# Third graph layer: other PSUM banks for the sums, another place for the keys, weights made in two parts, one more step in a tile's end

## The chip, the cores and the metric

The kernel runs on one core of a Trainium2 chip. The metric is the device time of one execution in microseconds; the kernel before has 2208.41 us, the median of three runs (2205.49 to 2208.99). The profile was taken in an execution of 2205.02 us whose span, from the first to the last instruction, is 2203.2 us. Times of day below, such as "1681.4", are microseconds from the start of that span.

## The reference

Four layers run one after the other over 4096 nodes with 128 features and one adjacency matrix of 4096 x 4096; each adds its result to x and normalises. The third and fourth (L2 and L3 of the reference) are the ones around the change:

```python
# layer 1: attention with 4 heads over adj, its output goes into x
x = _layernorm(x + _L1_gnn_ref(x, adj, Wq, bq, Wk, bk, Wv, bv, Ws, bs, Wb), axis=-1)

# layer 2: graph convolution
adj_hat = adj + eye(n)
d = (adj_hat.sum(1) + 1e-08) ** -0.5
x = _layernorm(x + relu(((d[:, None] * adj_hat * d[None, :]) @ x) @ weight))

# layer 3: graph attention with one head
H = x @ W.T + b
s, r = H @ a_s, H @ a_r
e = leaky_relu(A * s + A * r.T, 0.2)
att = softmax(where(A > 0, e, NEG), axis=1)
x = _layernorm(x + att @ H)
```

## The kernel before, in words

`layer1` is the attention. It keeps, in a pool `keep1` of SBUF, the values `VA` (17,024 bytes in a partition), the keys `KS` (64 KB), two buffers of queries `QS` and one of adjacency, `at0`, in this order. Its work is in one of two branches of a run-time If: `attention_unshifted`, which runs with these inputs, or `attention_shifted`. In the first, a step is one block of 128 keys against 512 queries: PE makes scores (L900), ACT the exponentials (L907), DVE masks them (L909), PE sums with the values (L926), the sums two steps behind the scores. When the 32 blocks of a tile of 512 queries are done, `ending` finishes the tile in pieces: ACT copies the two sums from PSUM (L939), PE transposes (L949), DVE and ACT do the rest and write `Y`, the scaled x of the tile (L1009). The last tile's `ending` has no scores beside it.

`layers23` follows at once. It opens a pool `ring` of 64 KB with eight slots of 1 MB of adjacency each, at the same SBUF address at which `keep1` began, then `keep3` and others behind it. Its PSUM pools `ps_a`, `ps_b`, `ps_t`, `ps_s` have two banks each, in this order from bank 0. In layer 1's branch that ran, `ps_s` (scores and the transposes `pto`) has banks 0 to 5 and `ps_v` (the sums) banks 6 and 7. In the other branch they belong to `ps_big` (0 to 3), `ps_t` (4 to 6) and `ps_o` (7), the last one for the sum `po`.

The loop over `groups` is written out by hand (`manual_schedule`), so the order in the code is the order on each engine. A block g is one slot of the ring; I = g // 8 is the tile of 512 output columns, J = g % 8 the block in it. For I < 8, `convolve` puts Y through the identity into the sum `pa` at J = 0 (L1254) and then adds four products with the block (L1260, two PE passes each, 8 matmuls in the trace). For J < 4, DVE also counts entries that are neither 0 nor 1 (`odd`, L1268). For the ninth tile, `attend_first` begins layer 3: DVE makes four weights `w` a block (L1280, four buffers) and PE sums them with `F` (L1283) into `pa3`.

Two pieces of work lie between the blocks. `weights`, after block 2, prepares layer 3's matrices: PE makes `pu` (L1224, L1225) and turns the weights into `pw` (L1234), DVE copies them out (L1228 to L1236), PE multiplies the copy by `last` into the same bank (L1237), DVE writes `wx`, `tot`, `eps` (L1238 to L1241). `finish(I)` ends tile I while tile I + 1 runs. It is a generator: its first piece, the copy of `pa` (L1297), goes out at J = 7, the others at J = 0, 1, 3, 5 and 6 of the next tile, after that block's own work:

- J = 0: product with the layer's weights (L1301), Relu on ACT (L1304), x + o on DVE (L1305), statistics, Ln and Exp of the variance (L1309, L1310)
- J = 1: normalisation of the four row groups (L1314)
- J = 3: transposes on PE (L1320), copy on ACT (L1321), `XB` on DVE (L1322)
- J = 5: products `pr` and `psr` (L1326, L1330), DVE and ACT make `rho` and `col`
- J = 6: `F` on ACT and DVE (L1344, L1345)

At the end of the loop `close_first` tests the ranges, PE adds the constant to `pa3` (L1386), ACT copies it to `a0` (L1387), the PSUM pools are closed, and a second If takes `attend_factored`. It opens `ps_a3` (two banks from 0) and `ps_b3` and runs layer 3 for the other seven tiles: PE L1425 opens a sum, DVE L1434 makes the `w`, PE L1437 adds.

A framework places tiles and pools and writes every semaphore wait itself: a new tile in reused memory waits for what used the memory before.

Of the kernel before, what the change touches and what calls it, by code (L numbers as in the profile page):

```python
# [10 lines left out]
F32R = mybir.dt.float32r  # L11
# [3 lines left out]
PSUM = bass.MemoryType.PSUM  # L15

P = 128
# [25 lines left out]
class Net:  # L43
# [701 lines left out]
    def layer1(self, Wq, bq, Wk, bk, Wv, bv, Ws, bs, Wb, R):  # L745
# [4 lines left out]
        nc, tc, N, NT, D, X = self.nc, self.tc, self.N, self.NT, self.D, self.X  # L750
        NH, C = 4, D // 4
        with ExitStack() as ctx:
            self.on_scalar = 4
            keep = ctx.enter_context(tc.tile_pool(name="keep1", bufs=1))

            VA = keep.tile([P, NT * NH * (C + 1) + 32], F32, tag="VA", name="VA")
            V = VA[:, 0 : NT * NH * (C + 1)].rearrange("p (t h c) -> p t h c", t=NT, h=NH)
            KS = keep.tile([P, NH, N], F32R, tag="KS", name="KS")
            QS = [keep.tile([P, NH, S], F32R, tag=f"QS{k}", name=f"QS{k}") for k in range(2)]
            at0 = keep.tile([P, 4, S], F32, tag="at0", name="at0")  # L760
            nc.scalar.dma_start(out=at0, in_=self.adjT[0, 0])
# [20 lines left out]
            with ExitStack() as pctx:  # L782
# [10 lines left out]
                for c in range(NC):  # L793
                    s = slice(c * S, (c + 1) * S)
                    for a, w, bias in ((1, wk, bkc), (0, wq, bqc)):
                        p = self.ps_t.tile([P, S], F32, tag="pt", name="pqk")
# [12 lines left out]
                for g in self.groups():  # L809
                    p = self.ps_t.tile([P, 4, P], F32, tag="pt", name="pt")  # L810
# [8 lines left out]
                for g in self.groups():  # L819
                    p = self.ps_t.tile([P, 4, P], F32, tag="pt", name="pt")  # L820
# [13 lines left out]
                p = self.ps_t.tile([P, S], F32, tag="pt", name="pb")  # L834
# [341 lines left out]
    def layers23(self, w2, weight, bias, a_s, a_r, out, Y):  # L1176
# [6 lines left out]
        with ExitStack() as ctx:  # L1183
# [3 lines left out]
            pctx = ctx.enter_context(ExitStack())  # L1187
# [9 lines left out]
            pre = pctx.enter_context(tc.tile_pool(name="pre3", bufs=1))  # L1197
            rot = pctx.enter_context(tc.tile_pool(name="rot2", bufs=2))
            wp = pctx.enter_context(tc.tile_pool(name="w2", bufs=4))
            ps_a = pctx.enter_context(tc.tile_pool(name="ps_a", bufs=2, space=PSUM))  # L1200
            ps_b = pctx.enter_context(tc.tile_pool(name="ps_b", bufs=2, space=PSUM))
            ps_t = pctx.enter_context(tc.tile_pool(name="ps_t", bufs=2, space=PSUM))
            ps_s = pctx.enter_context(tc.tile_pool(name="ps_s", bufs=2, space=PSUM))
            w = self.load_mat(w2, "w2")
            br = self.load_row(bias, "br3", keep)
            wn = self.load_mat(weight, "wn3", pre)
# [14 lines left out]
            def weights():  # L1221

                p = ps_t.tile([P, 4, P], F32, tag="pt", name="pu")
                nc.tensor.matmul(p[:, 0, 0:2], lhsT=wn, rhs=ac[:, 0:2], start=True, stop=True)  # L1224
                nc.tensor.matmul(  # L1225
                    p[:, 1, 0:2], lhsT=ac[:, 2:3].to_broadcast([P, P]), rhs=ac[:, 0:2], start=True, stop=True
                )
                nc.vector.tensor_copy(us, p[:, 0, 0:1].to_broadcast([P, P]))  # L1228
                nc.vector.tensor_copy(ur, p[:, 0, 1:2])
                nc.vector.tensor_copy(cb, p[:, 1, 0:2])  # L1230


                p = ps_t.tile([P, 4, P], F32, tag="pt", name="pw")
                nc.tensor.transpose(p[:, 0, :], wn, self.ident)  # L1234
                nc.vector.tensor_copy(wt, p[:, 0, :])
                nc.vector.tensor_copy(last, self.ident[:, D - 1 : D].to_broadcast([P, P]))  # L1236
                nc.tensor.matmul(p[:, 1, :], lhsT=last, rhs=wt, start=True, stop=True)  # L1237
                nc.vector.tensor_tensor(wx[:, 0:D], wt, p[:, 1, :], ALU.subtract)  # L1238
                nc.vector.tensor_copy(wx[:, D : D + 1], self.ident[:, D - 1 : D])
                nc.vector.memset(tot[:, D - 1 : D], float(N))  # L1240
                nc.vector.memset(eps, TINY)  # L1241
# [45 lines left out]
            def finish(I):  # L1287


                s, tl = slice(I * S, (I + 1) * S), slice(4 * I, 4 * I + 4)  # L1290
                x = X[:, tl, :]
                a = rot.tile([P, S], F32, tag="a", name="a")
                o = rot.tile([P, 4, D], F32, tag="o", name="o")
                rs = rot.tile([P, 4], F32, tag="rs", name="rs")
                XT = rot.tile([P, S], F32, tag="XT", name="XT")
                r = rot.tile([P, 4], F32, tag="r", name="r")
                nc.scalar.copy(a, st["pa"])  # L1297
                yield
                pb = ps_b.tile([P, 4, D], F32, tag="pb", name="pb")
                for b in range(4):  # L1300
                    nc.tensor.matmul(pb[:, b, :], lhsT=a[:, b * P : (b + 1) * P], rhs=w, start=True, stop=True)  # L1301
                for b in range(4):
                    t = 4 * I + b
                    nc.scalar.activation(o[:, b, :], pb[:, b, :], AF.Relu, scale=d[:, t : t + 1])  # L1304
                nc.vector.tensor_tensor(x, x, o, ALU.add)  # L1305
                for b in range(4):
                    self.row_stats(4 * I + b)
                nc.vector.tensor_scalar(rs, self.mv[:, tl, 1], EPS_LN, None, op0=ALU.add)
                nc.scalar.activation(rs, rs, AF.Ln)  # L1309
                nc.scalar.activation(rs, rs, AF.Exp, scale=-0.5)  # L1310
                yield
                for b in range(4):
                    t = 4 * I + b
                    nc.vector.tensor_scalar(  # L1314
                        X[:, t, :], X[:, t, :], self.mv[:, t, 0:1], rs[:, b : b + 1], op0=ALU.subtract, op1=ALU.mult
                    )
                yield
                p = ps_t.tile([P, 4, P], F32, tag="pt", name="pt")
                for b in range(4):
                    nc.tensor.transpose(p[:, b, :], X[:, 4 * I + b, :], self.ident)  # L1320
                nc.scalar.activation(XT, p.rearrange("p a b -> p (a b)"), AF.Identity, accum_out=part[:, I : I + 1])  # L1321
                nc.vector.tensor_tensor(XB[:, tl, :], x, br.unsqueeze(1).to_broadcast([P, 4, D]), ALU.add)  # L1322
                yield
                pr = ps_s.tile([P, S], F32, tag="ps", name="pr")
                for b in range(4):
                    nc.tensor.matmul(  # L1326
                        pr[:, b : b + 1], lhsT=XT[:, b * P : (b + 1) * P], rhs=ur, start=True, stop=True
                    )
                ps = ps_s.tile([P, S], F32, tag="ps", name="psr")
                nc.tensor.matmul(ps, lhsT=us, rhs=XT, start=True, stop=True)  # L1330

                nc.vector.tensor_scalar(r, pr[:, 0:4], cb[:, 1:2], 2.0 * LIMIT, op0=ALU.add, op1=ALU.min)
                nc.vector.tensor_scalar(r, r, -2.0 * LIMIT, None, op0=ALU.max)
                nc.vector.tensor_reduce(mx[:, I : I + 1], r, AX.X, ALU.max, apply_absolute_value=True)
                nc.vector.tensor_scalar(rho[:, s], ps, cb[:, 0:1], 2.0 * LIMIT, op0=ALU.add, op1=ALU.min)
                nc.vector.tensor_reduce(
                    mx[:, NS + I : NS + I + 1], rho[:, s], AX.X, ALU.max, apply_absolute_value=True
                )
                nc.scalar.activation(col[:, 0, tl], r, AF.Exp, scale=-0.8)
                nc.scalar.activation(col[:, 1, tl], r, AF.Exp)  # L1340
                nc.scalar.activation(rho[:, s], rho[:, s], AF.Exp, scale=0.8)
                yield
                for t in range(4 * I, 4 * I + 4):
                    nc.scalar.activation(F[:, t, 0 : D - 1], X[:, t, 0 : D - 1], AF.Copy, scale=col[:, 1, t : t + 1])  # L1344
                nc.vector.tensor_copy(F[:, tl, D - 1], col[:, 1, tl])  # L1345
# [19 lines left out]
            with tc.manual_schedule():  # L1365
                nc.scalar.preload_act_table_set("natural_log_exp_and_others")
                for g in range(RING - 1):
                    load(g)
                for g in range(groups):
                    I, J = g // NS, g % NS  # L1370
                    if I < NS:
                        convolve(I, J)
                    else:
                        attend_first(J)
                    load(g + RING - 1)
                    if g == 2:
                        weights()

                    if J in (0, 1, 3, 5, 6):
                        next(rest, None)  # L1380
                    if J == NS - 1 and I < NS:
                        rest = finish(I)
                        next(rest)
                    if g == groups - 2:
                        close_first()
                nc.tensor.matmul(st["pa3"], lhsT=tot, rhs=eps, start=False, stop=True, skip_group_check=True)  # L1386
                nc.scalar.copy(a0, st["pa3"])  # L1387
# [166 lines left out]
```

## Time and profile before

The stretches of the span around the change, from the profile's windows:

| stretch, us | what runs | PE busy, us | DVE busy, us | ACT busy, us | granted clock |
|---|---|---|---|---|---|
| 1660 to 1680 | last blocks of layer 1 | 15.93 | 17.01 | 10.83 | 1.00 |
| 1680 to 1700 | `ending` of the last tile, blocks 0 to 2 of layer 2 | 14.77 | 13.83 | 0.92 | 0.83 |
| 1700 to 1720 | `weights`, blocks 3 to 7 | 17.79 | 7.45 | 0.00 | 0.91 |
| 1745 to 1936 | tiles 1 to 7 of layer 2 | 191.00 | 91.87 | 45.22 | 1.00 |
| 1936 to 1985 | `attend_first` with `finish(7)` | 40.93 | 31.79 | 9.54 | 0.93 |
| 1985 to 2203.2 | `attend_factored` | 209.12 | 185.91 | 7.61 | 0.99 |

A row is read like this: in the 191 us from 1745 on, PE had a matmul in flight all the time, DVE was busy for less than half of it. The granted clock is the share of TensorE's full speed that the chip gave; at 0.5 every matmul takes twice as long. Over the whole span PE is busy 88%, DVE 85%, ACT 67%.

### The profile page before, as it was taken

To read this page: it belongs to the slowest core of one execution; us is meant where nothing else is said; L and a number is where in the kernel's file an instruction comes from. 1 tells how busy PE (TensorE), PEld (TensorE's weight loads), DVE (VectorE), ACT (ScalarE), POOL (GpSimd) and SP (SyncE) were. 2 spreads that over 40 slices of the span, in tenths; PEclk is the share of its full clock that TensorE was granted. 3 is DMA by queue.
4 is the path that set the end of the run, shared out by engine and by line. 5 is a ranking of instruction groups with operands and counts; after the bars stand their busy time and mean duration, and the time that the engine had idled before them with its cause. 6 is when DMAs were issued, how large, how long until landed. Compare 5 with 4: busy or idle time off the path is not lost.

```text
span 2203.2 us, 24053 instructions
## 1 busy us (share of the span) xinstructions
PE 1944.5 (88%) x8720; PEld 1051.3 (48%) x8720; DVE 1881.1 (85%) x2732; ACT 1474.4 (67%) x1858; POOL 97.8 (4%) x146
## 2 busy tenths in 40 slices
PE   4588888888888708999999999999997999989998
PEld 4376666666666505333333333333333444434443
DVE  6799999999999887789999999999897344558887
ACT  5799999999999774787777787877883222210000
POOL 2000000000000322210000000000000000000000
PEclk7799999999999857999999999999999999999999
DMA  3466665667566307885646565565455777667883
GB/s 93 139 225 224 207 225 202 232 211 247 207 210 215 116 1 248 215 227 174 203 158 187 174 201 178 173 191 176 169 195 222 293 269 272 254 235 275 290 297 112
DMA packets 112868, 448.44 MB, mean 204 GB/s; under 512 B 9760, under 2 KB 20064, under 8 KB 71776
## 3 DMA queue, kind: packets, MB, share of 16 engines
q1 hardware_dynamic: 94160, 361.82, 46.4%
q10 hardware_dynamic: 9360, 68.16, 9.1%
q0 software_dynamic: 9216, 16.78, 4.2%
q8 instruction: 73, 1.20, 0.2%
q14 instruction: 59, 0.48, 0.1%
HBM read 369.10 MB, written 77.63 MB: 203 GB/s over the span
## 4 chain that ended last, share of the span: by engine, by line
PE 40%; DVE 33%; ACT 20%; issue 5%; DMA 2%; ACTq 0%; POOL 0%; SPq 0%; DVEq 0%; POOLq 0%
PE pv L926 10%; PE pa L1260 10%; PE pa L1437 9%; DVE e L909 8%; PE ps L900 6%; ACT e L907 3%; ACT w L612 3%; DVE w L620 3%; DVE t L603 2%; DVE nat L890 2%; DVE w L652 2%; DVE t L648 2%; ACT at L584 2%; ACT y L630 2%; DVE w L663 2%
## 5 line engine op out<-in xcount | busy, mean ns | idle before, releaser
L909 DVE SCALAR_TENSOR_TENSOR e<-at,e 128x2048 f32<-128x2048 f32 x256 | 583.0, 2287 | 69.3 <-ACT e L907 68.6
L907 ACT ACTIVATE e<-ps 128x1024 f32<-128x1024 f32 x512 | 493.1, 1024 | 145.8 <-PE ps L900 126.0
L926 PE MATMUL pv<-e,VA 128*64 128x512 f32 x2048 | 495.8, 605 | 6.7 <-DVE e L909 6.3
L900 PE MATMUL ps<-QS,KS 128*128 128x512 f32 x1024 | 312.9, 424 | 5.1 <-ACT e L907 2.9
L900 PEld LDWEIGHTS ps<-QS,KS 128*128 128x128 f32 x1024 | 171.0, 189 | 230.7 <-ACT e L907 175.1
L926 PEld LDWEIGHTS pv<-e,VA 128*64 128x64 f32 x2048 | 124.7, 136 | 248.7 <-issue 214.3
L1260 PE MATMUL pa<-ring,Y 128*128 128x512 f32 x512 | 228.0, 599 | 1.4 <-DMA wn<-in_L_gnn_W_dram 1.4
L580 PE MATMUL ptA<-ident,ad 128*128 128x128 f32 x1024 | 158.8, 284 | 51.4 <-ACT at L584 48.2
L1437 PE MATMUL pa<-w,F 128*128 128x512 f32 x448 | 195.3, 594 | 0.0
L1434 DVE SCALAR_TENSOR_TENSOR w<-rho,col,ring 128x512 f32<-128x512 f32 x224 | 162.8, 748 | 24.0 <-PE pa L1437 11.3
L580 PEld LDWEIGHTS ptA<-ident,ad 128*128 128x128 f32 x1024 | 120.6, 144 | 130.0 <-ACT at L584 95.8
L596 PE MATMUL pz<-HT 128*128 128x512 f32 x288 | 152.2, 631 | 24.3 <-DVE w L663 15.8
L675 PE MATMUL pi<-HA,w 128*128 128x129 f32 x1152 | 158.6, 284 | 0.0
L1260 PEld LDWEIGHTS pa<-ring,Y 128*128 128x128 f32 x512 | 96.9, 193 | 115.1 <-issue 114.8
L675 PEld LDWEIGHTS pi<-HA,w 128*128 128x128 f32 x1152 | 146.5, 200 | 2.7 <-issue 2.3
L620 DVE TENSOR_TENSOR w<-w,at 128x2048 f32<-128x2048 f32 x64 | 146.4, 2287 | 0.5 <-ACT at L584 0.5
L1437 PEld LDWEIGHTS pa<-w,F 128*128 128x128 f32 x448 | 83.7, 190 | 106.1 <-issue 79.2
L881 ACT ACTIVATE nat<-nat 128x2048 f32<-128x2048 f32 x64 | 122.6, 1915 | 3.8 <-DMA nat<-in_adj_dram 3.7
L690 PE MATMUL pj<-HA,w 128*128 128x129 f32 x896 | 109.5, 274 | 2.4 <-DVE w L663 2.4
L603 DVE SCALAR_TENSOR_TENSOR t<-ei,de,pz 128x512 f32<-128x512 f32 x144 | 104.1, 745 | 6.8 <-DMA ei<-rows 6.7
L690 PEld LDWEIGHTS pj<-HA,w 128*128 128x128 f32 x896 | 104.6, 191 | 2.6 <-DVE w L663 2.6
L658 PE MATMUL ptz<-ident,t 128*128 128x128 f32 x448 | 69.8, 283 | 31.9 <-DVE w L663 22.9
(359 smaller groups left out, 2456.6 us busy)
## 6 DMA issues: line engine op xcount, KB each, us to landing
ring<-adjT SPq DMA_DIRECT2D x128, 1024.0 KB, 5.1
ad<-in_adj_dram SPq DMA_DIRECT2D x64, 1024.0 KB, 5.3
adjT<-at SPq DMA_DIRECT2D x64, 1024.0 KB, 5.0
nat<-in_adj_dram ACTq DMA_DIRECT2D x64, 1024.0 KB, 4.9
at<-adjT SPq DMA_DIRECT2D x63, 1024.0 KB, 4.8
qk<-cut SPq DMA_DIRECT2D x16, 512.0 KB, 11.7
KS<-qk POOLq DMA_DIRECT2D x32, 256.0 KB, 7.1
QS<-qk POOLq DMA_DIRECT2D x32, 256.0 KB, 5.3
```

The source lines that it names most:

```text
L580: nc.tensor.transpose(pt[:, ib, :], ad[:, ib, jb * P : (jb + 1) * P], self.ident)
L596: nc.tensor.matmul(pz, lhsT=HT[:, j * P : (j + 1) * P], rhs=HT[:, I * S : (I + 1) * S], start=True, stop=True)
L620: nc.vector.tensor_tensor(w, w, st[p][f"at{k}"], ALU.mult)
L675: nc.tensor.matmul(row[I, "po"][ib // 2][:, ib % 2, :], lhsT=st[p]["w0"][:, jb, ib * P : (ib + 1) * P], rhs=HA[:, 4 * J + jb, :], start=False,
L690: nc.tensor.matmul(pj[:, a, :], lhsT=st[p]["w1"][:, ib, jb * P : (jb + 1) * P], rhs=HA[:, 4 * I + ib, :], start=(ib == 0), stop=(ib == 3),)
L900: nc.tensor.matmul(p[:, h, :], lhsT=KS[:, h2 + h, jb * P : (jb + 1) * P], rhs=QS[I % 2][:, h2 + h, :], start=True, stop=True,)
L907: nc.scalar.activation(e[:, h2 : h2 + 2, :], p, AF.Exp)
L909: nc.vector.scalar_tensor_tensor(e, at[:, jb % 4, :].unsqueeze(1).to_broadcast([P, NH, S]), 0.0, e, op0=ALU.not_equal, op1=ALU.mult,)
L926: nc.tensor.matmul(st["po"][h // 2][g : g + 64, :], lhsT=VA[:, o : o + 64], rhs=e[:, h, :], start=(jb == 0), stop=(jb == NT - 1), skip_gro ...
L1260: nc.tensor.matmul(st["pa"], lhsT=Y[:, 4 * J + jb, :], rhs=at[:, jb, :], start=False, stop=(J == NS - 1 and jb == 3), skip_group_check=True,)
L1434: nc.vector.scalar_tensor_tensor(w, rho[:, I * S : (I + 1) * S], col[:, 0, j : j + 1], at[:, jb, :], op0=ALU.max, op1=ALU.mult)
L1437: nc.tensor.matmul(pa, lhsT=F[:, j, :], rhs=w, start=False, stop=(j == NT - 1), skip_group_check=True)
```

## The change

There are four edits. In layer 1, `KS` is allocated ahead of `VA`, so that the ring of adjacency afterwards lies over the keys, whose last use is before that of the values. In `layers23` the pool of the sums, `ps_a`, comes last of the four PSUM pools, so it has banks 6 and 7, and layer 3's `ps_a3`, again from bank 0, no longer lies over it. `weights` is cut in two: what needs PE's second product goes into `weights_last`, after block 4, with other blocks between the copies and the product. `finish` gets one more `yield`, after the Relu, so that DVE's part of the first piece comes one block later; the pieces now go out at J = 0, 1, 2, 3, 5 and 6.

```diff
@@ layer1
             keep = ctx.enter_context(tc.tile_pool(name="keep1", bufs=1))
+            KS = keep.tile([P, NH, N], F32R, tag="KS", name="KS")
             VA = keep.tile([P, NT * NH * (C + 1) + 32], F32, tag="VA", name="VA")
...
-            KS = keep.tile([P, NH, N], F32R, tag="KS", name="KS")
@@ layers23
-            ps_a = pctx.enter_context(tc.tile_pool(name="ps_a", bufs=2, space=PSUM))
             ps_b = pctx.enter_context(tc.tile_pool(name="ps_b", bufs=2, space=PSUM))
             ps_t = pctx.enter_context(tc.tile_pool(name="ps_t", bufs=2, space=PSUM))
             ps_s = pctx.enter_context(tc.tile_pool(name="ps_s", bufs=2, space=PSUM))
+            ps_a = pctx.enter_context(tc.tile_pool(name="ps_a", bufs=2, space=PSUM))
@@ weights
                 nc.vector.tensor_copy(last, self.ident[:, D - 1 : D].to_broadcast([P, P]))
+                st["pw"] = p
+
+            def weights_last():
+                p = st["pw"]
                 nc.tensor.matmul(p[:, 1, :], lhsT=last, rhs=wt, start=True, stop=True)
                 nc.vector.tensor_tensor(wx[:, 0:D], wt, p[:, 1, :], ALU.subtract)
@@ finish
                     nc.scalar.activation(o[:, b, :], pb[:, b, :], AF.Relu, scale=d[:, t : t + 1])
+                yield
                 nc.vector.tensor_tensor(x, x, o, ALU.add)
@@ the loop over groups
                     if g == 2:
                         weights()
-
-                    if J in (0, 1, 3, 5, 6):
+                    if g == 4:
+                        weights_last()
+
+                    if J in (0, 1, 2, 3, 5, 6):
                         next(rest, None)
```

## The prediction

> **What bounds the kernel now.** I read the page first: PE is busy 88% and leads the chain of waits with 40% of the span, DVE follows with 33%. Such shares mix stages, so I then asked for stretches of the part that the diff touches, from the end of layer 1 (about 1676 us) to the end.
>
> ```profile
> 1697.60:1702.20 4.60, 0.01 (x1) 0.00 (x0) 4.52 (x9) 0.00 (x0) 0.00 (x0) 0.99 1.01 422
> 1702.20:1705.60 3.40, 3.39 (x6) 1.84 (x7) 2.51 (x5) 0.00 (x0) 0.00 (x0) 0.51 1.01 424
> 1745.00:1936.00 191.00, 191.00 (x571) 94.81 (x572) 91.87 (x179) 45.22 (x110) 0.00 (x0) 1.00 0.72 267
> 1936.00:1950.50 14.50, 9.95 (x31) 4.74 (x29) 6.12 (x18) 5.48 (x13) 0.00 (x0) 1.00 0.65 250
> 1950.50:1962.60 12.10, 12.10 (x25) 5.20 (x26) 11.27 (x19) 1.01 (x2) 0.00 (x0) 0.86 0.60 204
> ```
>
> After the length come PE, PEld, DVE, ACT and POOL busy, then the granted clock. Most of layer 2 (1745 to 1936) has no PE gap: no edit can win there unless it shortens PE's own work, and none does. What can be won lies in the seams: 4.6 us without PE at 1697.6, the hole before 1950.5, and the stretches right behind both, where the clock is 0.51 and 0.86. The timeline names the waits at the first seam:
>
> ```profile
> 1677.41 0.32 SPq L1244 DMA_DIRECT2D ring<-adjT  x1
> ...
> 1681.41 1.83 PE L1254 MATMUL pa<-ident,Y 128*128 128x128 f32 x8 [3.97 <-DVE junk L967]
> ...
> 1684.67 12.43 PE L1260 MATMUL pa<-ring,Y 128*128 128x512 f32 x24 [1.42 <-DMA wn<-in_L_gnn_W_dram]
> ...
> 1687.49 0.21 ACT L994 ACTIVATE rs<-rs 128x4 f32<-128x4 f32 x1
> ...
> 1702.21 0.80 PE L1237 MATMUL pw<-wtr,last 128*128 128x128 f32 x2 [4.60 <-DVE last L1236]
> ...
> 1702.80 18.70 PE L1260 MATMUL pa<-ring,Y 128*128 128x512 f32 x40
> ```
>
> and at the seam between layers 2 and 3:
>
> ```profile
> 1947.14 0.69 DVE L1305 TENSOR_TENSOR X<-X,o 128x512 f32<-128x512 f32 x1 [8.17 <-ACT o L1304]
> ...
> 1949.68 2.74 DVE L1280 SCALAR_TENSOR_TENSOR w<-rho,col,ring 128x512 f32<-128x512 f32 x4
> ...
> 1950.48 12.26 PE L1283 MATMUL pa<-w,F 128*128 128x512 f32 x24 [4.55 <-DVE w L1280]
> ...
> 1962.59 0.60 PE L1320 MATMUL pt<-ident,X 128*128 128x128 f32 x4
> ...
> 1985.70 0.58 ACT L1387 COPY a<-pa 128x512 f32<-128x512 f32 x1 [5.45 <-PE pa L1386]
> ...
> 1986.38 1.09 PE L1425 MATMUL pa<-eps,tot 1*128 1x512 f32 x2 [0.72 <-ACT a L1387]
> ```
>
> The brackets hold the idle time before a piece and what ended it. Strange is the first one: L1254 reads Y and the identity, yet waits for `junk`, which it never touches. I come back to that.
>
> **What the Trainium skill says.** "TensorE: Matmul & The Clock Gate", Part 1: the clock drops to half after an idle window of about 3.4 us and comes back after a busy one, and the windows run freely. The trace agrees: 0.51 for the 3.4 us after the 4.6 us gap, and the weight loads of L1260 there stand 0.85 us apart instead of 0.43. So a gap of PE costs itself plus about 1.7 us. "PSUM: Partial Sum Buffer", section "Engine vs sequencer instructions": the queues of ScalarE and VectorE are strict FIFO. Agreed: the `w` of L1280 stand behind L1305 for 8.17 us with nothing to wait for themselves. "Runtime: NRT & Kernel Launch", section "Instruction fetch mechanics": a taken branch to a far target stalls for the fetch. The trace has PE's branch at the end of layer 1's If with 3.47 us from 1676.8, so PE is free at 1680.3; what it then waits for is a semaphore.
>
> **The change part by part.**
>
> *Keys ahead of values in `keep1`.* `ring` then covers exactly KS, whose last reader is the last L900 (ends 1669.5), and no more VA, read by L926 until 1676.1. If the first ring load waited for just what lies below it, it could go some 7.8 us earlier than 1677.41. But the wait list of that load, in the instructions that the framework emitted for the kernel before, also holds the last read of `at0` and the loads of QS0 and QS1. Those lie beyond 140352 bytes, the ring between 57792 and 123328. So the wait is for the whole pool `keep1`, VA with it, in whatever order the tiles lie. Also, PE needs ring[0] only at 1683.24 (1681.41 + 1.83); earlier landing could win 1.42 at most. I take 0; both ends: 0 and -1.4.
>
> *PSUM order.* `ps_a` moves from banks 0 and 1 to 6 and 7; `ps_b`, `ps_t`, `ps_s` move down by two. At layer 3's entry `ps_a3` lies in banks 0 and 1, until now those of `pa3`, which a0's copy (L1387) still reads. In the new order they are `ps_b`'s, idle since 1946. PE's wait of 0.72 before L1425 goes: -0.7, on PE's path, since layer 3 has PE busy 209 of 218 us.
>
> At layer 2's entry it is the other way round. The waits after the If are the larger of what its two branches ask: L1254 waits for DVE ticks that in the other branch, `attention_shifted`, are the last writes of Y, and in the branch that ran happen to be `junk` (L967). That explains the odd bracket, and the first ring load waiting for `pto` (L949), which in the other branch is VA's last reader. Bank 7 is, in that branch, `po`, last read by a ScalarE copy with tick 1473. In the branch that ran, tick 1473 is L994, which ends at 1687.70. Banks 0 and 1 have no such reader. So L1254 must wait until about 1687.8 instead of 1681.4. With its 1.83 us the first L1260 starts at 1689.6 instead of 1684.67: 4.9 later. It loses less to the clock, because the idle gap inside 1681 to 1685 is gone: before, 24 matmuls took 12.43 instead of 3 x 3.44 = 10.3, so 2.1 lost; now the half clock should last until some 1691.7 (the windows of before run on), of which 2.1 us fall on L1260, about 1.0 lost. Net +3.9. Behind L1254 on PE stands all of layer 2, so this lies on the path. Bounds: 0 if no such wait is made, +6.9 if it is for the branch's last DVE instruction (ends 1689.6).
>
> *Weights in two parts.* The matmul L1237 waits for the copies of L1228 to L1236, and these stand in DVE's queue behind three `odd` of 2.29 us each that start at 1694.5. PE ends L1234 at 1697.6 and gets to L1260 at 1702.80, then 40 matmuls take 18.70 instead of 17.2: 5.2 + 1.5 = 6.7 in all. With L1237 after block 4, PE has two blocks, 6.9 us, to run meanwhile. Even starting 3.9 later it reaches block 3 at 1701.6 and L1237 at about 1708.5, while `last` is written at 1702.2 as before: no wait. The pair of matmuls itself stays, about 0.4. So -6.3. Blocks 3 and 4 are there by then: their loads are issued by 1689.4, and the longest landing of a ring load was 14.2 us. The other copies (wx, tot, eps) fill DVE time at block 4, where it has no `odd`.
>
> *A tile's end in one more piece.* For I of 0 to 6 nothing: PE has no gap there, and X's normalisation (L1314, at 1827.0 to 1828.1 in one tile) comes after `odd` already and would still be ahead of the transposes at 1831.2, with 3 us to spare. For I = 7 it counts. Now L1305 waits for o until 1947.14 and holds up the second block's `w`; with the extra step these four go ahead, limited only by the four buffers, which PE frees from 1942.3 to 1945. PE then runs block 1 from 1945.9 to 1949.4. L1305 and the statistics end at 1949.7 as before, then come block 2's `w`; PE waits 1.1 (1949.4 to 1950.45), too short for the clock to fall. Normalisation 1952.4 to 1953.5, block 3's `w` from there, PE waits 0.3, block 3 ends at 1957.7 and the transposes stand there instead of at 1962.59: -4.9. The rest keeps its order (pr at J = 5, F at J = 6), with its waits of 2.2 and 1.3, so I carry -4.8 to the end. Bounds: 0 if another wait takes the place, -5.5 if even the new ones vanish.
>
> Sum: +3.9 - 6.3 - 4.8 - 0.7 = -7.9, from 2208.4 to 2200.5.
>
> **The rivals.** *A, no late start:* the wait for tick 1473 isn't made, or has long passed. Against it: the ticks from the unused branch are visible in two waits of this trace. For it: no PSUM wait of that kind shows in the trace of before, I only infer it. Then -11.8: 2196.6, and 2195.2 if the ring also comes earlier. *B, the tile's end wins nothing:* `w`, F and col of the last tile hang on a chain through ACT, DVE and PE, and the extra step could push the normalisation behind the transposes. Against it stand the 4 us between 1953.5 and 1957.7. Then -3.1: 2205.3. *C, slower:* layer 2 starts 6.9 late, and the weights' gap was only a place where DVE caught up: `odd` or a ring block then stops PE elsewhere, and the last tile gives nothing. +6.9 - 0.7 = 2214.6. Against it: PE is never held by the ring between 1705 and 1936, and DVE is busy only 92 of 191 us.
>
> **How the numbers follow.** Forecast 0.60, A 0.22, B 0.11, C 0.07. The runs of before spread over 3.5 us, so I give each case about 2 either way. The range leaves out C, the upper part of B and a little of A below: 2194.8 to 2205.5. Faster by over 0.2% means below 2204.0: nearly all of the forecast, all of A, a quarter of B: 0.82. Slower means above 2212.8: most of C, 0.05. The rest is 0.13.
>
> **What would show it.** In the changed kernel's timeline: L1254 starting at about 1687.8 behind ACT's L994 (right) or at 1681.4 (A); the first ring load still right behind L949; no gap of PE before L1237; `w` of block 1 ahead of L1305 and the transposes of the last tile some 16 us after the last block of layer 2 instead of 21; no wait for L1387 before L1425. I am wrong if layer 2's middle shows gaps of PE, or if the ring's first load comes before 1675.

## The result, and the profile after

The changed kernel takes 2198.07 us (median; 2194.3 to 2199.6) against 2207.51 us of the kernel before in the same session: ratio 0.9955, 95% interval [0.9938, 0.9973], 9.4 us faster. The forecast was 2200.5 us. A second session gave 2198.62 against 2208.48 us, 0.9963 [0.9950, 0.9977]. The spans of the two profiles differ by 8.4 us, 2203.2 and 2194.8.

Line numbers shift a little in the changed file: before's L1254, L1260, L1237, L1280, L1283, L1305, L1320, L1386, L1425 are now L1258, L1264, L1241, L1284, L1287, L1310, L1325, L1393, L1432; in e3, e4, e6 and e8 some stand a line or a few beside these. First the windows of the changed kernel (length, then busy time of PE, PEld, DVE, ACT and POOL, granted clock, DMA):

```profile
1676.10:1687.90 11.80, 1.39 (x11) 0.86 (x9) 9.98 (x54) 1.27 (x5) 0.00 (x0) 0.72 0.75 263
1687.90:1701.40 13.50, 13.50 (x37) 7.21 (x38) 8.76 (x14) 0.23 (x2) 0.00 (x0) 0.87 0.96 380
1701.40:1708.30 6.90, 6.90 (x19) 3.07 (x18) 2.96 (x7) 0.00 (x0) 0.00 (x0) 1.00 1.00 417
1745.00:1933.00 188.00, 188.00 (x564) 93.38 (x563) 89.49 (x174) 44.92 (x108) 0.00 (x0) 1.00 0.75 267
1933.00:1947.90 14.90, 13.84 (x39) 6.31 (x37) 9.49 (x23) 5.42 (x13) 0.00 (x0) 1.00 0.79 292
1947.90:1955.20 7.30, 7.25 (x17) 3.04 (x18) 7.30 (x14) 1.08 (x2) 0.00 (x0) 1.00 0.67 230
```

The middle of layer 2 is as full as it was. The gap in the weights is gone (1701.4 to 1708.3 is all PE, at full clock), and so is the larger part of the gap in the last tile's end. But a new hole stands in the first row: PE works 1.39 of 11.8 us. The list of PE's waits between 1660 and 1990 names all of them, first in the kernel before (who waited for whom, us in total, times, longest),

```profile
PE pa L1283 <- DVE w L1280: 8.1, 3, 4.6
PE pw L1237 <- DVE last L1236: 4.6, 1, 4.6
PE pa L1254 <- DVE junk L967: 4.0, 1, 4.0
PE pa L1260 <- DMA wn<-in_L_gnn_W_dram: 1.4, 1, 1.4
...
PE pa L1425 <- ACT a L1387: 0.7, 1, 0.7
```

then in the changed one:

```profile
PE pa L1258 <- ACT rs L994: 10.3, 1, 10.3
PE pa L1287 <- DVE w L1284: 4.6, 3, 2.2
PE pv L926 <- DVE e L909: 1.4, 2, 1.0
```

The wait for `last` and that for a0's copy have left the list, the waits for `w` have gone from 8.1 to 4.6, and the wait at the start of layer 2 has grown from 4.0 to 10.3, with another name behind it. The timeline of the changed kernel answers to the lines shown of before:

```profile
1677.56 0.32 SPq L1248 DMA_DIRECT2D ring<-adjT  x1
...
1687.88 2.08 PE L1258 MATMUL pa<-ident,Y 128*128 128x128 f32 x8 [10.29 <-ACT rs L994]
1689.75 11.32 PE L1264 MATMUL pa<-ring,Y 128*128 128x512 f32 x24
...
1708.29 0.38 PE L1241 MATMUL pw<-wtr,last 128*128 128x128 f32 x2
1708.51 4.03 PE L1264 MATMUL pa<-ring,Y 128*128 128x512 f32 x9
```

```profile
1938.92 3.60 PE L1287 MATMUL pa<-w,F 128*128 128x512 f32 x8
...
1939.98 3.33 DVE L1284 SCALAR_TENSOR_TENSOR w<-rho,col,ring 128x512 f32<-128x512 f32 x4 [3.54 <-PE pa L1287]
...
1944.61 0.69 DVE L1310 TENSOR_TENSOR X<-X,o 128x512 f32<-128x512 f32 x1 [1.31 <-ACT o L1308]
...
1947.95 7.38 PE L1287 MATMUL pa<-w,F 128*128 128x512 f32 x16 [1.11 <-DVE w L1284]
1955.16 0.60 PE L1325 MATMUL pt<-ident,X 128*128 128x128 f32 x4
...
1966.61 5.40 PE L1287 MATMUL pa<-w,F 128*128 128x512 f32 x8 [2.22 <-DVE w L1284]
...
1977.12 1.12 PE L1393 MATMUL pa<-eps,tot 1*128 1x512 f32 x2
1978.08 1.02 PE L1432 MATMUL pa<-eps,tot 1*128 1x512 f32 x2
```

DVE now makes the `w` of block 1 ahead of `x + o` (L1310). The last tile's transposes stand 16.2 us behind the first product with `F`, before it was 21.1 (1941.45 to 1962.59). L1432 follows L1393 with no bracket at all.

Totals of these kernels spread by some 4 us from run to run, and the same point of the program is reached several microseconds earlier or later because of the layers ahead. So I measure each profile in three stretches that start and end at PE instructions: **layer 2**, from the transposes L949 of layer 1's last tile to the first product with `F` (L1283); **tile end**, from there to L1386; **layer 3**, from there to the end of the span. The lines named are those of the kernel before; two columns give where L1254 and the first L1260 stand behind L949.

| kernel | L949 to L1254 | L949 to first L1260 | layer 2 | tile end | layer 3 |
|---|---|---|---|---|---|
| before | 5.40 | 8.66 | 265.44 | 43.09 | 218.66 |
| after | 11.73 | 13.60 | 262.77 | 38.20 | 217.68 |
| e1_unused_branch | 5.40 | 7.23 | 257.18 | 36.51 | 217.69 |
| e2_only_banks | 11.73 | 13.59 | 263.85 | 44.14 | 217.76 |
| e3_only_weights | 5.40 | 7.90 | 258.04 | 43.10 | 220.43 |
| e4_only_end | 5.39 | 7.23 | 265.23 | 39.44 | 218.70 |
| e5_banks_2_3 | 5.40 | 7.24 | 256.14 | 38.22 | 217.76 |
| e6_keys_pool | 5.74 | 7.58 | 257.94 | 39.46 | 217.69 |
| e7_products_split | 5.39 | 7.23 | 257.61 | 34.03 | 217.71 |
| e8_best | 5.54 | 7.38 | 256.30 | 34.03 | 217.77 |
| e9_only_keys | 5.39 | 7.23 | 264.35 | 43.77 | 220.38 |
| e10_after_again | 11.72 | 13.59 | 262.39 | 38.21 | 217.87 |

### The profile page after: what moved, and what is told of

Same layout as the page of the kernel before. It is cut to its first block, busy times and chain, and to the rows that moved or that the text cites. A ratio compares the mean times of both kernels' runs of the same rounds, so it can differ in the third digit from the quotient of the medians.

```text
span 2194.8 us, 24059 instructions
## 1 busy us (share of the span) xinstructions
PE 1936.8 (88%) x8720; PEld 1043.1 (48%) x8720; DVE 1880.6 (86%) x2732; ACT 1474.8 (67%) x1858; POOL 97.8 (4%) x146
## 4 chain that ended last, share of the span: by engine, by line
PE 41%; DVE 35%; ACT 17%; issue 5%; DMA 2%; POOL 0%; ACTq 0%; SPq 0%; DVEq 0%; POOLq 0%
PE pa L1264 10%; PE pv L926 9%; DVE e L909 9%; PE pa L1444 9%; PE ps L900 6%; ACT e L907 4%; DVE w L620 4%; ACT w L612 3%; DVE t L603 2%; DVE nat L890 2%; DVE w L652 2%; DVE t L648 2%; DVE w L663 2%; DVE at L584 1%; DVE t L640 1%
## 5 line engine op out<-in xcount | busy, mean ns | idle before, releaser
L1264 PE MATMUL pa<-ring,Y 128*128 128x512 f32 x512 | 225.7, 594 | 0.0
L1441 DVE SCALAR_TENSOR_TENSOR w<-rho,col,ring 128x512 f32<-128x512 f32 x224 | 162.7, 745 | 22.9 <-PE pa L1444 10.3
L596 PE MATMUL pz<-HT 128*128 128x512 f32 x288 | 152.8, 633 | 23.3 <-DVE w L663 16.2
L675 PE MATMUL pi<-HA,w 128*128 128x129 f32 x1152 | 153.6, 278 | 0.6 <-DVE w L652 0.6
L1264 PEld LDWEIGHTS pa<-ring,Y 128*128 128x128 f32 x512 | 95.9, 191 | 111.5 <-issue 111.3
L675 PEld LDWEIGHTS pi<-HA,w 128*128 128x128 f32 x1152 | 141.4, 194 | 3.8 <-issue 2.3
```

Source lines behind the costliest of these rows:

```text
L596: nc.tensor.matmul(pz, lhsT=HT[:, j * P : (j + 1) * P], rhs=HT[:, I * S : (I + 1) * S], start=True, stop=True)
L675: nc.tensor.matmul(row[I, "po"][ib // 2][:, ib % 2, :], lhsT=st[p]["w0"][:, jb, ib * P : (ib + 1) * P], rhs=HA[:, 4 * J + jb, :], start=False,
L1264: nc.tensor.matmul(st["pa"], lhsT=Y[:, 4 * J + jb, :], rhs=at[:, jb, :], start=False, stop=(J == NS - 1 and jb == 3), skip_group_check=True,)
L1441: nc.vector.scalar_tensor_tensor(w, rho[:, I * S : (I + 1) * S], col[:, 0, j : j + 1], at[:, jb, :], op0=ALU.max, op1=ALU.mult)
```

## The experiments

**e10: how far the same kernel moves.** The changed kernel again, with no edit.

> The changed kernel once more, on the chip of e9_only_keys. Theory: as measured the first time, 0.9955 of before. It shows how far the same kernel's total and its three stretches (262.8, 38.2 and 217.7) move from one profile to the next; half-clock windows should move them by up to 1.7 us each.

Measured: 262.39, 38.21 and 217.87, within 0.4 us of the first profile. Other rows that should be alike show jumps: the tile end is 36.51 in e1 and 39.44 in e4 against 38.2. Behind the same gap of 2.2 us, the same eight products took 5.40 us in the changed kernel and in e10, but in e1 and in e4

```profile
1964.09 3.70 PE L1287 MATMUL pa<-w,F 128*128 128x512 f32 x8 [2.23 <-DVE w L1284]
...
1968.06 6.63 PE L1283 MATMUL pa<-w,F 128*128 128x512 f32 x8 [2.22 <-DVE w L1280]
```

For e4 the windows show the clock there:

```profile
1968.00:1974.70 6.70, 6.64 (x10) 2.70 (x10) 2.62 (x9) 1.18 (x5) 0.00 (x0) 0.55 0.46 157
```

The clock is 0.55 over 6.7 us; in the changed kernel it is half for about 3.4 us, in e1 not at all. So a stretch is good to some 1.5 us, and to much less where no gap of PE lies in it.

**e1: the late start is a wait for a branch that never runs.** Edit on the changed kernel, in `attention_shifted`:

```diff
-                nc.scalar.copy(junk[:, 2, :], po)
+                nc.vector.tensor_copy(junk[:, 2, :], po)
```

> The changed kernel with one line altered in attention_shifted, the branch of layer 1 that does not run: DVE instead of ACT copies the sum po out of PSUM. Theory (the late start of layer 2 is a wait for a tick that only the unused branch needs): L1258 starts at about 1681.5 behind L967 instead of at 1687.9 behind L994, the first L1264 at about 1684.7; from L949 to the first L1287 some 258.8 us instead of 262.8; in all about 12 us less than the kernel before. Rival (the wait comes from what the branch that runs did with banks 6 and 7): L1258 still at 1687.9, 8 to 9 us less than before.

Measured: 2195.62 against 2207.92 us, ratio 0.9949 [0.9932, 0.9966], layer 2 in 257.18 instead of 262.77, and in the timeline

```profile
1684.05 0.08 DVE L967 DVE_READ_ACCUMULATOR junk<-Y,wb 128x1 f32 x1
...
1684.62 1.62 PE L1258 MATMUL pa<-ident,Y 128*128 128x128 f32 x6 [3.96 <-DVE junk L967]
```

The instructions that ran are the same ones. One line in code that was jumped over moved the start of layer 2 by 6.3 us; the rival, a wait on layer 1's own use of the banks, is out. The totals of the two kernels come from different sessions and their intervals overlap, so what it is worth, 5.6 us of layer 2, rests on the stretch.

**e2: the banks alone.** Edit on the kernel before: `ps_a` opened last, as in the change.

> The kernel before with ps_a moved to the end of the PSUM pools alone. Theory: L1254 starts at 1687.9, 6.5 later, but the late start hides behind DVE, whose copies for L1237 end at about 1702.2 all the same; PE's gap before L1237 shrinks from 4.6 to about 1 us, too short for the half clock, so block 3 begins at about 1702.7 at full clock. From L949 to the first L1283 some 264 us instead of 265.4, from L1386 to the end 217.7 instead of 218.7: 2 to 3 us faster than before. Rival (the parts add up): 3.9 later, 0.7 won: 3 us slower than before.

Measured: 2206.23 against 2207.92 us, ratio 0.9993 [0.9984, 1.0002]. The total can't be told from no change, and 2 to 3 us had been expected; the rival's 3 us slower lies outside the interval. The first seam shows why:

```profile
1687.88 2.08 PE L1254 MATMUL pa<-ident,Y 128*128 128x128 f32 x8 [10.29 <-ACT rs L994]
1689.74 11.47 PE L1260 MATMUL pa<-ring,Y 128*128 128x512 f32 x24
...
1702.40 0.49 PE L1237 MATMUL pw<-wtr,last 128*128 128x128 f32 x2 [0.68 <-DVE last L1236]
1702.72 9.61 PE L1260 MATMUL pa<-ring,Y 128*128 128x512 f32 x22
```

PE starts 6.3 us later and then waits 0.68 instead of 4.60 for `last`: both times it leaves that point at 1702.7 or 1702.8, now with no half clock behind it. Here the late start costs nothing, because DVE holds PE at the next point anyway. The two runs with undivided weights and an early start that follow below, e4 and e9, show the same from the other side. PE comes to L1237 earlier and waits longer:

```profile
1701.26 0.80 PE L1237 MATMUL pw<-wtr,last 128*128 128x128 f32 x2 [7.18 <-DVE last L1236]
...
1703.06 0.80 PE L1237 MATMUL pw<-wtr,last 128*128 128x128 f32 x2 [5.71 <-DVE last L1236]
```

Layer 2 is 1.6 shorter, as expected; layer 3 is 0.9 shorter. The tile end, which the edit doesn't touch, is 1.05 longer: behind the same gap of 4.55 us the 24 products took 13.30 instead of 12.26, again a longer half clock.

**e3: the weights alone.** Edit on the kernel before: `weights_last` after block 4.

> The kernel before with the weights in two parts alone. Theory: no gap before L1241 and no half clock behind it; from L949 to the first L1287 some 259 us instead of 265.4, the rest as before: about 6.3 us faster. Rival (the gap comes back at block 4, or the ring's blocks are not there): 262 or more, less than 3 us faster.

Measured: 2200.11 against 2207.92 us, ratio 0.9966 [0.9953, 0.9978]; layer 2 in 258.04, 7.4 shorter; PE has no wait at L1241:

```profile
1705.04 0.38 PE L1241 MATMUL pw<-wtr,last 128*128 128x128 f32 x2
```

The 7.4 include 0.8 less at the first L1260, where the kernel before waited 1.42 for a transfer and this one 0.46.

**e4: the tile's end alone.** Edit on the kernel before: the `yield` behind the Relu, and J = 2 in the list.

> The kernel before with the one more yield in finish and its step at J = 2 alone. Theory: nothing in layer 2 (265.4 from L949 to the first L1283), 38.2 us instead of 43.1 from the first L1283 to L1386: 4.9 us faster. Rival (the last tile's gain needs the other edits, or layer 2's tiles lose by a later normalisation): 41 or more there, or over 266 in layer 2.

Measured: 2203.07 against 2207.92 us, ratio 0.9981 [0.9974, 0.9988]; layer 2 as before at 265.23; tile end 39.44, of which 1.2 is the longer half clock shown above. The last tile's gain needs no other edit.

**e9: the keys alone.** Edit on the kernel before: `KS` ahead of `VA`.

> The kernel before with KS ahead of VA alone. Theory (waits are for whole pools): the first ring load goes 1.4 us behind the start of L949 as before, L1254 at 5.4, from L949 to the first L1283 about 265.4: no difference to the kernel before. Rival (the ring waits for what lies below it): first ring load some 6.5 us ahead of L949, up to 1.4 us faster.

Measured: 2208.3 against 2208.48 us, ratio 1.0000 [0.9991, 1.0008]. The first ring load goes 1.40 us behind the start of L949, as before: alone, this edit changes nothing that can be measured.

**e5: both gains at once.** Edit on the changed kernel:

```diff
             ps_b = pctx.enter_context(tc.tile_pool(name="ps_b", bufs=2, space=PSUM))
+            ps_a = pctx.enter_context(tc.tile_pool(name="ps_a", bufs=2, space=PSUM))
...
-            ps_a = pctx.enter_context(tc.tile_pool(name="ps_a", bufs=2, space=PSUM))
```

> The changed kernel with ps_a second instead of last of the PSUM pools, so the sums have banks 2 and 3. In the unused branch these belong to ps_big, which only DVE reads, and in layer 3 to ps_b3, not ps_a3. Theory: both gains at once: L1258 5.4 us after L949 as in the kernel before, from L949 to the first L1287 257 to 259 us instead of 262.8, and still no wait of L1432 for the copy to a0; about 12 us less than before. Rival (banks 2 and 3 make layer 3's first products pb wait for a0's copy): L1418 held at the second block, 0.7 us or more lost there.

Measured: 2193.33 against 2208.84 us, ratio 0.9927 [0.9914, 0.9941]; 12 us had been expected, the medians differ by 15.5. Layer 2 in 256.14, layer 3 in 217.76: the early start and the free entry into layer 3 together, and no price for it in layer 3.

```profile
1686.18 2.04 PE L1258 MATMUL pa<-ident,Y 128*128 128x128 f32 x8 [3.96 <-DVE junk L967]
1688.02 11.06 PE L1264 MATMUL pa<-ring,Y 128*128 128x512 f32 x24
...
1976.10 1.02 PE L1432 MATMUL pa<-eps,tot 1*128 1x512 f32 x2
```

**e6: an early ring.** Edit on e5:

```diff
+            kp = ctx.enter_context(tc.tile_pool(name="keys1", bufs=1))
+            KS = kp.tile([P, NH, N], F32R, tag="KS", name="KS")
             keep = ctx.enter_context(tc.tile_pool(name="keep1", bufs=1))
-            KS = keep.tile([P, NH, N], F32R, tag="KS", name="KS")
```

> e5_banks_2_3 with KS in a pool of its own ahead of keep1, so that the ring lies over this pool alone. Theory (waits are for whole pools): the first ring load now goes some 6.5 us ahead of L949, right behind the last scores, instead of 1.4 behind it. But PE is held by the ticks of Y, so the first ring product starts 7.2 us after L949 as in e1_unused_branch; 0 to 1.4 us won over e5_banks_2_3, not to be told from none by the total. Rival (the ring's first block is what layer 2 waits for): that product starts 4 us or more earlier, and the total falls by as much.

Measured: 2194.56 against 2208.84 us, ratio 0.9940 [0.9926, 0.9954], next to e5's 0.9927. In the timeline three loads go ahead of L950 (L949 before):

```profile
1669.71 1.27 SPq L1249 DMA_DIRECT2D ring<-adjT  x3
```

and the queue's wait is now for the scores:

```profile
SPq L1249 <- PE ps L901: 18.5, 1, 18.5
```

So what the edit of the change was for can be had, by a pool instead of an order in a pool. It is worth nothing: the first product with the ring stands at 7.58 us, not 4 us earlier. In e5 PE doesn't wait for the ring either (no bracket at L1264), so there was nothing to win.

**e7: one more piece in the tile's end.** Edit on e5:

```diff
                 nc.tensor.matmul(ps, lhsT=us, rhs=XT, start=True, stop=True)
+                yield
...
-                    if J in (0, 1, 2, 3, 5, 6):
+                    if J in (0, 1, 2, 3, 4, 5, 6):
```

> e5_banks_2_3 with one more yield in finish, behind the products pr and psr, which now go out at J = 4, and DVE's part of them at J = 5. Theory (PE's gap of 2.2 us before block 6 in the last tile is DVE waiting in order for pr and psr, with w behind them): the gap goes and with it the half clock; from the first L1287 to the sum's last product about 34.5 us instead of 38.2; nothing elsewhere. Rival (DVE has 4.8 us of work for that block against PE's 3.4, so it is just late): a gap of 1 us or more stays before block 6, 36 or more.

Measured: 2189.49 against 2208.84 us, ratio 0.9914 [0.9900, 0.9927]; tile end 34.03. DVE makes `w` of block 5 before it turns to `r`, and then no longer waits for `pr`:

```profile
1950.63 5.92 DVE L1284 SCALAR_TENSOR_TENSOR w<-rho,col,ring 128x512 f32<-128x512 f32 x8
1956.58 0.22 DVE L1337 TENSOR_SCALAR r<-pr,cb 128x4 f32<-128x4 f32 x1
```

and PE runs blocks 5 and 6 with no gap between them:

```profile
1957.34 7.03 PE L1287 MATMUL pa<-w,F 128*128 128x512 f32 x16
```

Of the 4.2 us against e5's 38.22, 2.2 are the gap and 1.7 the half clock behind it. As that half clock varies, the gain is 2.5 against e1's 36.51 and 5.4 against e6's 39.46. The intervals of the totals of e5 and e7 overlap, so the gain rests on the stretch.

**e8: both together.** e5 with the edits of e6 and e7.

> e5_banks_2_3 with both the keys in their own pool and the products of finish split. Theory: the sum of the two, 15 to 17 us less than before, about 2191 to 2193. Rival (the two meet in the same wait): no more than the better of the two.

Measured: 2188.04 against 2208.84 us, ratio 0.9906 [0.9891, 0.9921], with a tile end of 34.03 like e7's. The interval overlaps e7's, so the pool for the keys adds nothing that can be told, and the sum that was expected wasn't one; the medians differ by 20.8, where 15 to 17 had been expected. Both e7 and e8 beat the kernel before by some 20 us and, by intervals that lie clear, the changed kernel too; e7 is the simpler.

## Why the prediction was right

**Keys and ring: right.** Taken at 0; e9 gives 1.0000, and the load stood where it had stood. e6 shows the reason given: with a pool of its own the wait is for the keys alone.

**Late start of layer 2: right in cause, in place and in time; its size depends on the other edits.** L1258 started at 1687.88 behind L994 where 1687.8 was written, the first L1264 at 1689.75 for 1689.6, block 3 at 1701.41 for 1701.6. e1 shows the cause. Against the profile of before, the first three blocks end 3.8 later behind L949, for a forecast 3.9. But in that profile PE waited 1.42 for a transfer ahead of the first L1260, and of the eight other profiles with an early start only e3 has such a wait, of 0.46. Layer 2 took 257.2 on the average of the six with divided weights and an early start (e1, e3, e5, e6, e7, e8) and 262.6 in the two of the changed kernel: with divided weights the late start costs 5.4. The reason given, that all of layer 2 stands behind L1254 on PE, holds only there. With undivided weights (e2) the late start costs nothing.

**Weights in two parts: right, with a remark on the sum.** PE had no wait at L1241, at 1708.29 for a forecast 1708.5. Layer 2 took 265.0 on the average of the three profiles with undivided weights and an early start (before, e4, e9). So the edit brings 7.8 to an early start, where 6.3 was forecast, and to a late one 1.3 (e2's 263.85 against 262.6). The two edits touch the same microseconds, so neither has a worth of its own. Measured with the weights first they come to -7.8 + 5.4, with the banks first to -1.2 - 1.3, both about -2.4; the forecast's +3.9 - 6.3 is -2.4 too, and the stretch went from 265.44 to 262.77, -2.7. Both terms of the forecast were thus some 1.5 too small, and in the sum this cancels. The likely source, not tested by a run of its own, is that both were read from the one profile with the wait of 1.42: that wait came out of PE's wait for `last`, 4.60 there against 7.18 in e4 and 5.71 in e9.

**Tile's end: right.** -4.8 forecast, 43.09 to 38.20 is -4.9; on the average of all profiles without and with the edit (e7 and e8 aside) it is 43.5 to 38.3, -5.2. The new waits of PE were to be 1.1 and 0.3; the trace shows 1.11, and the two blocks behind it take 7.38 instead of 7.03. One reading was too simple: during the 8.17 ahead of L1305 the `w` did have something to wait for at first, a free buffer. In the changed kernel they start 1.06 behind the first product with `F`, which in the kernel before would have been at 1942.5; only the 4.6 from there to 1947.14 were L1305's doing.

**Entry into layer 3: right in cause, too small in size.** Forecast -0.7, measured 218.66 to 217.68, -1.0: besides the wait of 0.72, L1393 and L1432 now overlap by 0.16. In e3 and e9, which keep the old banks, this stretch took 220.4, and the clock was 0.81 and 0.80 in the 9 us behind the entry instead of 1.00; in e4, with the old banks too, it took 218.70. So in two of four profiles that small gap came with a half clock soon behind it, in none of the eight without the gap, and then removing it is worth 2.7.

**The clock: right where it counted, too simple as a rule.** The prediction took from the Trainium skill, "TensorE: Matmul & The Clock Gate", Part 1, that the clock falls after an idle window of about 3.4 us, and from the trace a price of 1.7 us for a gap. The measurement differs and decides: a gap of 2.2 us was enough in nine of the ten profiles that have it, and cost 0, 1.7 or 2.9 us besides itself (eight products in 3.70, 5.40 or 6.63 us). The forecast that the new gap of 1.1 us would be too short came true: the clock is 1.00 in the 7.3 us from 1947.9.

In sum -7.9 was forecast, and the spans differ by 8.4, the medians by 9.4. Rivals A, B and C didn't come: A would have needed L1258 at 1681.4, B no gain in the tile's end, C gaps in the middle of layer 2.

## What to carry to other kernels

Where a framework writes the waits, ask what a buffer's place was used for in every branch of an If, not just in the one that runs, and whether it waits for tiles or for whole pools; a name in a wait that is no operand of the waiting instruction is the sign. Before you add up edits at one seam, find out who holds the engine at the next point: a late start of 6 us was free there with one edit and cost 5 with another. In a loop in which an in-order engine makes the next block's input, put one block between a product and the part of that engine that waits for it; this gave 5 and then some 4 us.

## What the runs showed that I had not expected

The same gap of PE does not always cost the same. Behind the gap of 2.2 us the clock stayed full once, was half for about 3.4 us seven times, and for longer twice, so that this gap alone moved the tile's end between 36.51 and 39.46. A gap of 0.72 at the entry into layer 3 cost now 1.0, now 2.7.
